# A decoder layer on one core: a second chain at the start, an earlier combine, a pipelined end, and another order of the first loads

## The chip, the cores and the metric

One core of one Trainium2 chip runs the whole kernel. Its engines work beside each other, each through its own list of instructions in order: TensorE (PE in the profile) multiplies and transposes, VectorE (DVE) and ScalarE (ACT) work on elements, GpSimd (POOL) makes masks, takes powers and issues indirect transfers, SyncE (SP) issues most other transfers. An instruction that waits for another engine or a transfer holds up everything behind it in its own list. The metric is the device time of one execution in microseconds, a median over runs.

## The reference, cut to what matters

The input x is 64 sequences of 128 tokens with 256 features; everything is float32.

```python
# 1. selective state space layer, residual twice, then a layernorm
xn = layernorm(x, gamma, beta)
x_inner, z = split(xn @ W_in, 2)              # 256 -> 2 * 512
x_conv = silu(conv1d(x_inner, conv_w) + conv_b)   # 4 taps, causal
Bmat, Cmat, delta = split(x_conv @ W_x)       # 16, 16, 1; delta = softplus
y = selective_scan(x_conv, -exp(A_log), Bmat, Cmat, delta)
y = (y + x_conv * D_skip) * silu(z)
x1 = norm(x + y @ W_out + x)
# 2. retention against a context, decay mask and rotation
qh, kh, vh = xpos(x1 @ Wq), xpos(ctx @ Wk), ctx @ Wv
x2 = norm(x1 + ((qh @ kh.T) * mask) @ vh)
# 3. experts: one shared, and 2 of 8 routed for each token
shared = (silu(x2 @ Wg) * (x2 @ Wu)) @ Wd
probs = sigmoid(x2 @ router_w.T + bias)       # top 2, scores to sum 1
routed = sum over the 2 of score * ((silu(x2 @ Wg[e]) * (x2 @ Wu[e])) @ Wd[e])
out = norm(x2 + shared + routed)
```

## The kernel before

The 64 sequences are taken in 16 groups (NG) of 4 (GB), 512 tokens to a group (T). All routed rows go through two arrays in device memory: route scatters each token's row twice into xs, sorted by expert, and the rows of products are scattered into ys by token.

What a group goes through is written as generators that yield between stretches of work. first_half(g) is front (layernorm, two transposes to xnT, the projections by w_in in two parts of four, between them the convolution on DVE and ScalarE's silu, then w_x and the softplus of delta) and scan (the selective scan as matmuls over chunks: pin and pof, pmt, the transposes to xd, the products with mt). In front, sz holds silu(z); scan multiplies it into the result, called acc. second_half(g) is after (w_out, layernorm, the retention with kh, qh and v, layernorm), route (router, top 2, places of the rows, scatters) and, when a batch of groups is complete, tile_list, which counts rows (a small product of ones and count) and lists the tiles of that batch. A tile is 256 rows (128 in the last batch) of one expert: one_tile fetches rows (rows_in<-xs) and weights, transposes, multiplies by gate and up (routed_gu), and the down product (routed_d) of the tile before; its rows go to ys. early_shared(g) is the shared expert of a group while the loop runs (L1029): hidden products, DVE's product hc, down products, the sum into x2, and a store to x2_rows.

The order of the program is made by the generators themselves: abreast takes, among several chains, always the one that is the least far on in a scale of ticks, and a chain's yield says how long its own next step should be held back. Tick g holds first_half(g), second_half(g-1), the early shared expert of g-2, and per_tick tiles of the batches listed by then (L1421). Each engine then runs its instructions in that order. A group's front waits at the free test (L632) until the group before has been read by after, because there is one sz buffer.

The seven groups in LATE (L42, groups 7 to 13) have no shared expert in the loop: route stores their x2 and its transpose, and late_shared (L1470) makes it at the end. After the loop a second abreast runs the rest of the tiles beside the shared expert of group 15, called the late tiles below, and a third, the end stage, runs late_shared for the late groups beside combine (L1242) for all 16: load the pair of product rows (picked<-ys), two adds on DVE, layernorm, store. combine runs first on the groups whose sums stand in memory.

At the start (L1536 and on) x of group 0 is loaded from POOL's queue; three small loads of A_log go on SP's, and the others on ScalarE's, w_in among the first. A comparison of A_log's rows makes a flag, and a branch (L1612 and on) picks shared_decay, which this input takes, or any_decay, which it doesn't. Exponentials of A_log (a_neg, a_row, a_col, L1587) stand on ScalarE in front of the last nine loads. After the branch, the first three steps of group 0's front are emitted (L1308), then the constants: masks on POOL, two half masks transposed on PE (L1345), the shared weights' load, tables of numbers.

layernorm (L552) is bn_stats and bn_aggr on DVE for each sequence, var, rstd on POOL, shift on DVE, and four norms on ScalarE.

Of the kernel before, what the change touches and what calls it, by code (L numbers as in the profile page):

```python
# [16 lines left out]
P = 128  # L17
# [27 lines left out]
LATE = range(7, 14)  # L45
# [8 lines left out]
def _any_decay(ctx, K):  # L54
# [77 lines left out]


    xts = [K.x0] + [const.tile([P, GB, D], F32, name=f"xt{i}") for i in range(2)]
# [375 lines left out]
def _shared_decay(ctx, K):  # L510
# [39 lines left out]
    xts = [K.x0] + [const.tile([P, GB, D], F32, name=f"xt{i}") for i in range(2)]  # L550

    def layernorm(dst, src):  # L552

        mv = small.tile([P, GB, 2], F32, name="mv")
        for b in range(GB):
            st = small.tile([P, nc.vector.BN_STATS_DIM], F32, name="st")
            nc.vector.bn_stats(st, src[:, b, :])  # L557
            nc.vector.bn_aggr(mv[:, b, :], st)  # L558
        var = small.tile([P, GB], F32, name="var")
        nc.vector.tensor_scalar(var, mv[:, :, 1], EPS, None, ALU.add)  # L560
        rstd = small.tile([P, GB], F32, name="rstd")
        nc.gpsimd.tensor_tensor(rstd, var, mhalf, ALU.pow)  # L562
        shift = small.tile([P, GB], F32, name="shift")
        nc.vector.scalar_tensor_tensor(shift, mv[:, :, 0], -1.0, rstd, ALU.mult, ALU.mult)  # L564
        yield 4.2
        for b in range(GB):
            nc.scalar.activation(  # L567
                dst[:, b, :], src[:, b, :], AF.Identity, bias=shift[:, b : b + 1], scale=rstd[:, b : b + 1]
            )
# [36 lines left out]
    def front(st):  # L606
# [3 lines left out]
        xn = one.tile([P, GB, D], F32, name="xn", tag="xn")  # L610
        yield from layernorm(xn, xt)
        yield 2.6
        xnT = one.tile([P, KD, T], F32, name="xnT", tag="xnT")
# [3 lines left out]
        xc = one.tile([P, CI, GB, L], F32, name="xc")  # L617
# [18 lines left out]
        sz = one.tile([P, CI, T], F32, name="sz")  # L636
# [15 lines left out]
        bcs = one.tile([P, T // 2], F32, name="bcs", tag="bcs")  # L652
        nc.scalar.copy(bcs, pbc)
        rows = dram.tile([2 * NS, T], F32, name="rows")
# [8 lines left out]
        tok = small.tile([P, GB, NX], F32, name="tok", bufs=1)  # L663
# [4 lines left out]
        bj = one.tile([KB, T], F32, name="bj")  # L668
        cj = one.tile([KB, T], F32, name="cj")
# [12 lines left out]
        cq = one.tile([P, GB, NS, Q], F32, name="cq", tag="xnT")  # L682
# [6 lines left out]
        raw = small.tile([P, GB], F32, name="raw", bufs=1)  # L689
        nc.vector.tensor_copy(raw, tok[:, :, NX - 1])  # L690
        e = small.tile([P, GB], F32, name="e", bufs=1)
# [3 lines left out]
        up = small.tile([P, GB], F32, name="up", bufs=1)  # L695
        nc.vector.tensor_scalar(up, e, 1.0, None, ALU.add)
        lg = small.tile([P, GB], F32, name="lg", bufs=1)
        nc.scalar.activation(lg, up, AF.Ln)

        dd = small.tile([P, GB], F32, name="dd", bufs=1)  # L700
        nc.vector.tensor_scalar(dd, up, 1.0, None, ALU.subtract)
        flat = small.tile([P, GB], F32, name="flat", bufs=1)
# [7 lines left out]
        dl = small.tile([P, GB], F32, name="dl", bufs=2)  # L710
# [3 lines left out]
    def scan(st):  # L714
# [5 lines left out]
        d1 = small.tile([P, GB, Q], F32, name="d1", bufs=1)  # L720
# [3 lines left out]
        dlb = small.tile([P, GB, 32], F32, name="dlb", bufs=1)  # L724
# [4 lines left out]
        eq = one.tile([P, GB, NS, Q], F32, name="eq", tag="xn")  # L729
# [11 lines left out]
        eb = one.tile([KB, T], F32, name="eb", tag="bcs")  # L741
# [14 lines left out]
        gq = small.tile([P, GB, Q], F32, name="gq", bufs=1)  # L756
        nc.vector.tensor_reduce(gq, eq.rearrange("p b n i -> p b i n"), AX.X, ALU.add)
        mt = one.tile([P, GB, NQ, Q], F32, name="mt", tag="dm")
# [7 lines left out]
        xd = [one.tile([P, 2, DI], F32, name=f"xd{j}", tag=tag) for j, tag in enumerate(("xnT", "xd"))]  # L766
# [21 lines left out]
    def after(g, st):  # L788
# [59 lines left out]
        x1T = one.tile([P, KD, T], F32, name="x1T")  # L848
# [61 lines left out]
    def route(g, st):  # L910
# [53 lines left out]
        rows = [st["row"], one.tile([P, GB, DX], F32, name="row1")]  # L964
# [38 lines left out]
    def shared(x2, x2T, x2s):  # L1003
# [3 lines left out]
        wd = shared_w[:, 2 * SZ :].rearrange("p (c h) -> p c h", c=CF)  # L1007
        hid = []
        for c in range(CF):
# [4 lines left out]
            hc = ring.tile([P, T], F32, name="hc", bufs=4)  # L1014
# [3 lines left out]
            yield 0.3 if c < CF - 1 else 2.0  # L1018
        for j in range(GB // 2):
            ps = gu.tile([P, 2, D], F32, name="gu")  # L1020
# [6 lines left out]
            yield  # L1027

    def early_shared(g, st):  # L1029
        yield from shared(st["x2"], st["x2T"], st["x2"])  # L1030
        nc.sync.dma_start(out=x2_rows[g].rearrange("p (b d) -> p b d", d=D), in_=st["x2"])

    def load_rows(g):
# [3 lines left out]
        return t  # L1037

# [97 lines left out]
    def fetch(i):  # L1136
# [16 lines left out]
        there.append(work[0] + 12.0)  # L1153
# [88 lines left out]
    def combine(g, x2s):  # L1242

        y = late.tile([P, GB, 2, D], F32, name="picked", bufs=3)
        nc.sync.dma_start(
            out=y, in_=ys[g * GB * 2 * L : (g + 1) * GB * 2 * L, :].rearrange(
                "(b p k) d -> p b k d", p=P, k=2)
        )
        yield 1.0
        for k in range(2):  # L1250
            nc.vector.tensor_tensor(x2s, x2s, y[:, :, k, :], ALU.add)  # L1251
        yield 3.0
        yield from layernorm(x2s, x2s)
        nc.sync.dma_start(out=out[g * GB : (g + 1) * GB].rearrange("b l d -> l b d"), in_=x2s)
# [49 lines left out]
    for before, st in zip([{"read": True}] + states, states):  # L1304
        st["free"] = lambda before=before: "read" in before
    states[0]["xt"] = xts[0]
    start = first_half(states[0])
    for _ in range(3):  # L1308
        next(start)

# [37 lines left out]
    for side in range(2):  # L1348
        t = one.tile([P, KB // NS, NS], F32, name=f"half{side}", tag="dm")
# [9 lines left out]
        ps = pm.tile([KB, P], F32, name="pm")  # L1359
        turn(ps, t.rearrange("p j n -> p (j n)"), ident)  # L1360
        tT = const.tile([KB, P], F32, name=f"halfT{side}")
        nc.vector.tensor_copy(tT, ps)
        halvesT.append(tT)
# [3 lines left out]
    shared_w = const.tile([P, 3 * SZ], F32, name="shared_w")  # L1367
    nc.sync.dma_start(out=shared_w, in_=ffn[0])
# [47 lines left out]
    for i in range(NW):  # L1416
        weights.append([const.tile([P, 2 * SZ], F32, name=f"routed_gu{i}"), const.tile([P, SZ], F32, name=f"routed_d{i}")])
    zeros = const.tile([P, DX], F32, name="zeros")
# [5 lines left out]
    for k, (groups, first, n, _) in enumerate(BATCHES[:-2]):  # L1424
        ticks = range(groups + 1, BATCHES[k + 1][0] + 1)
        for j, t in enumerate(ticks):
            per_tick[t] = n * (j + 1) // len(ticks) - n * j // len(ticks)
    def until(ready, at):
# [3 lines left out]
    def first_halves():  # L1432
        for g in range(NG):
            if g + 1 < NG:
                yield from until(lambda: g < 2 or "read" in states[g - 2], g)
                states[g + 1]["xt"] = load_x(g + 1)
            yield from placed(first_half(states[g]) if g else start, g, 54.0)
            states[g]["scanned"] = True

# [24 lines left out]
    abreast((first_halves(), True), (second_halves(), True), (shared_ones(), True), (tiles_beside(), True))  # L1464
# [5 lines left out]
    def late_shared(g):  # L1470
        x2 = load_rows(g)
        x2T = two.tile([P, KD, T], F32, name="x2T")
        nc.sync.dma_start(out=x2T.rearrange("p k t -> p (k t)"), in_=x2T_rows[g])
        yield 4.0
        x2s = late.tile([P, GB, D], F32, name="x2s_late", bufs=len(LATE))
        yield from shared(x2, x2T, x2s)
        sums.append((g, x2s))

    sums = []
# [10 lines left out]
    sums += [(g, None) for g in range(NG) if g not in LATE]  # L1490

    def all_sums():
        for i in range(NG):
            while not sums:
                yield i / NG, 1.0
            g, x2s = sums.pop(0)
            yield from placed(combine(g, load_rows(g) if x2s is None else x2s), i / NG, 12.0, 1 / NG)

    def all_shared():
        for i, g in enumerate(LATE):  # L1500
            yield from placed(late_shared(g), i / len(LATE), 27.0, 1 / len(LATE))
# [5 lines left out]
def decoder_layer(  # L1507
# [29 lines left out]
    nc.gpsimd.dma_start(out=x0, in_=x[0:GB].rearrange("b l d -> l b d"))  # L1537
# [42 lines left out]

    gam, bet = column(gamma, "gam"), column(beta, "bet")
    w_in_s = chunked(w_in, 2 * DI, "w_in_s")
    cw, cb = chunked(conv_w, TAPS, "cw"), column(conv_b, "cb")
# [105 lines left out]
```

## Time and profile before

| what | value |
| --- | --- |
| median of 3 runs | 1994.55 us (1994.12 to 1998.49) |
| the profiled execution | 1992.64 us |
| its span | 1990.8 us |
| mean granted PE clock | 0.986 |
| the late tiles, from the last batch's count to the last tile | 1516 to 1819.5 us of the span |
| the end stage | 1819.5 to 1976.3 us |
| the tail, behind the last matmul | 1976.3 to 1990.8 us |

The span is the stretch that the profile shows, from the first to the last work of the core; the execution's own time has 1.84 us around it. In the page, "PE" is the matmuls and "PEld" the loads of their stationary operand, which overlap; a float32 matmul is shown as two records. A wait names the engine that waited, the line it waited at, and what released it. In a group of records, "out<-in" are the names of the buffers.

The page's slices show the shape of the execution: PE is busy from the second slice on, DVE half the time in the loop, little among the late tiles, and more in the end stage, where the transfers are the densest:

```profile
PE   4889998999999979999999899999998999999996
DVE  3666766655565554555555645554532111113573
DMA  4111121431502123313251324152103433443772
GB/s 144 32 56 45 43 73 38 159 93 32 158 25 93 32 87 127 114 55 107 62 158 51 120 60 140 48 167 56 54 27 117 135 133 125 163 166 127 271 252 74
```

### The profile page before, as it was taken

How to read it: one execution, taken by the hardware profiler on the slowest of the kernel's cores; microseconds unless marked ns; L12 is line 12 of the kernel's file. 1: busy time of each engine (PE TensorE's matmuls, PEld its weight loads, DVE VectorE, ACT ScalarE, POOL GpSimd, SP SyncE). 2: the span in 40 equal slices, each digit the busy share in tenths (PEclk: the TensorE clock that was granted, in tenths of full speed). 3: DMA queues.
4: the chain of work that ended last, by engine and by line, in shares of the span. 5: the costliest groups of instructions: out<-in, count | busy, mean ns of one | idle time of the engine just before them, and what ended most of it. 6: DMA issues, size and time to landing. Idle time of an engine off the chain costs nothing. (4 is left out here: it accounts for less than half of the span.)

```text
span 1990.8 us, 26551 instructions
## 1 busy us (share of the span) xinstructions
PE 1873.7 (94%) x9252; PEld 1393.7 (70%) x9252; DVE 990.8 (50%) x2398; ACT 757.8 (38%) x1248; POOL 470.2 (24%) x711
## 2 busy tenths in 40 slices
PE   4889998999999979999999899999998999999996
PEld 2655665685868666767677677687776888997554
DVE  3666766655565554555555645554532111113573
ACT  3345445243434323535444434445331222222332
POOL 3031220231303031413141313131214222222010
PEclk9899999999999989999999999999999999999998
DMA  4111121431502123313251324152103433443772
GB/s 144 32 56 45 43 73 38 159 93 32 158 25 93 32 87 127 114 55 107 62 158 51 120 60 140 48 167 56 54 27 117 135 133 125 163 166 127 271 252 74
DMA packets 100775, 200.14 MB, mean 101 GB/s; under 512 B 22840, under 2 KB 60344, under 8 KB 96024
## 3 DMA queue, kind: packets, MB, share of 16 engines
q1 hardware_dynamic: 77512, 143.08, 22.9%
q0 software_dynamic: 17616, 52.46, 7.7%
q10 hardware_dynamic: 5504, 2.81, 0.5%
q8 instruction: 75, 1.23, 0.3%
q14 instruction: 68, 0.56, 0.1%
HBM read 207.33 MB, written 58.60 MB: 134 GB/s over the span
## 5 line engine op out<-in xcount | busy, mean ns | idle before, releaser
L543 PE MATMUL gu<-rows_T,routed_gu 128*128 128x256 f32 (+1 forms) x2496 | 501.9, 352 | 0.0
L543 PEld LDWEIGHTS gu<-rows_T,routed_gu 128*128 128x128 f32 x2496 | 416.7, 191 | 59.3 <-issue 16.5
L1203 DVE TENSOR_TENSOR hid<-hid,gu 128x512 f32<-128x512 f32 x135 | 92.4, 685 | 360.6 <-PE gu L543 256.6
L543 PE MATMUL pm<-routed_d,hid 128*128 128x256 f32 x1080 | 254.7, 381 | 0.3
L543 PE MATMUL pm<-xnT,w_in_s 128*128 128x512 f32 x512 | 242.0, 598 | 4.5 <-ACT xnT L580 2.7
L1219 POOL DMA_INDIRECT ys<-rows_out,to x135 | 140.8, 1043 | 406.9 <-ACT rows_out L1218 360.5
L543 PE MATMUL gu<-x2T,shared_w 128*128 128x512 f32 x512 | 229.7, 595 | 0.2
L543 PEld LDWEIGHTS pm<-routed_d,hid 128*128 128x128 f32 x1080 | 199.3, 190 | 26.4 <-issue 2.5
L628 DVE SCALAR_TENSOR_TENSOR xc<-pm,cw,xc 128x508 f32<-128x508 f32 (+2 forms) x192 | 140.9, 739 | 65.3 <-ACT xc L623 62.2
L543 PEld LDWEIGHTS gu<-x2T,shared_w 128*128 128x128 f32 x512 | 94.8, 190 | 108.4 <-issue 101.9
L543 PEld LDWEIGHTS pm<-xnT,w_in_s 128*128 128x128 f32 x512 | 95.5, 192 | 90.1 <-issue 76.6
L567 ACT ACTIVATE x<-x,shift,rstd 128x256 f32<-128x256 f32 x132 | 70.7, 592 | 204.9 <-DVE shift L564 204.9
L562 POOL TENSOR_TENSOR rstd<-var,mhalf 128x4 f32<-128x4 f32 x64 | 67.6, 1056 | 330.1 <-DVE mv L558 175.2
L1218 ACT ACTIVATE rows_out<-pm,wt 128x256 f32<-128x256 f32 x135 | 58.0, 472 | 205.3 <-PE pm L543 193.2
L543 PE MATMUL gu<-shared_w,hc 128*128 128x256 f32 x512 | 118.6, 386 | 8.1 <-DVE hc L1016 8.1
L1202 ACT ACTIVATE hid<-gu 128x512 f32<-128x512 f32 x135 | 80.4, 596 | 112.6 <-PE gu L543 102.4
L543 PE MATMUL pm<-w_out_s,sz 128*128 128x256 f32 x512 | 117.7, 382 | 5.3 <-DVE sz L784 4.9
L543 PEld LDWEIGHTS gu<-shared_w,hc 128*128 128x128 f32 x512 | 96.8, 192 | 29.7 <-DVE hc L1016 12.6
L543 PEld LDWEIGHTS pm<-w_out_s,sz 128*128 128x128 f32 x512 | 95.8, 190 | 27.6 <-DVE sz L784 9.8
L992 POOL DMA_INDIRECT xs<-x,index x64 | 66.7, 1043 | 173.4 <-DVE row L988 80.3
L623 ACT ACTIVATE xc<-pm,cb,cw 128x512 f32<-128x512 f32 x64 | 49.7, 777 | 116.7 <-PE pm L543 116.7
L1015 ACT ACTIVATE hc<-gu 128x512 f32<-128x512 f32 x64 | 37.9, 593 | 117.7 <-PE gu L543 109.6
(233 smaller groups left out, 2505.6 us busy)
## 6 DMA issues: line engine op xcount, KB each, us to landing
routed_gu<-in_ffn_dram SPq DMA_DIRECT2D x78, 1024.0 KB
routed_d<-in_ffn_dram SPq DMA_DIRECT2D x78, 512.0 KB
picked<-ys SPq DMA_DIRECT2D x16, 1024.0 KB
rows_in<-xs SPq DMA_DIRECT2D x57, 258.0 KB
cT<-in_ctxT_dram POOLq DMA_DIRECT2D x16, 512.0 KB
cq<-chunks SPq DMA_DIRECT2D x16, 512.0 KB
x_rows<-x SPq DMA_DIRECT2D x16, 512.0 KB
xt<-in_x_dram POOLq DMA_DIRECT2D x10, 512.0 KB
```

What stands on the lines that cost most here:

```text
L543: nc.tensor.matmul(out, lhsT=lhsT, rhs=rhs, **how)
L562: nc.gpsimd.tensor_tensor(rstd, var, mhalf, ALU.pow)
L567: nc.scalar.activation(dst[:, b, :], src[:, b, :], AF.Identity, bias=shift[:, b : b + 1], scale=rstd[:, b : b + 1])
L623: nc.scalar.activation(xcf[:, c, :], ps, AF.Identity, bias=cb[:, c : c + 1], scale=cw[:, c, TAPS - 1 : TAPS],)
L628: nc.vector.scalar_tensor_tensor(xc[:, c, :, s:], ps3[:, :, : L - s], cw[:, c, TAPS - 1 - s : TAPS - s], xc[:, c, :, s:], ALU.mult, ALU.add,)
L992: s = nc.gpsimd.indirect_dma_start(out=xs, in_=rows[k][:, b, :], in_offset=None, out_offset=bass.IndirectOffsetOnAxis(ap=index[:, b, k : k ...
L1015: nc.scalar.activation(hc, psg, AF.Silu)
L1202: nc.scalar.activation(hc, psg, AF.Silu)
L1203: nc.vector.tensor_tensor(hc, hc, psu, ALU.mult)
L1218: nc.scalar.activation(y[:, j, :], ps[:, j, :], AF.Copy, scale=wt[:, j : j + 1])
L1219: s = nc.gpsimd.indirect_dma_start(out=ys, in_=y[:, j, :], in_offset=None, out_offset=bass.IndirectOffsetOnAxis(ap=to[:, j : j + 1], axis=0),)
```

## The change

In parts. The late groups are 7 to 12 in place of 7 to 13, and one tile fewer is placed in the last tick of the loop:

```diff
-LATE = range(7, 14)
+LATE = range(7, 13)
...
+    per_tick[NG] -= 1
...
-        there.append(work[0] + 12.0)
+        there.append(work[0] + (12.0 if i >= NW and shape(i - NW)[0] == k else 24.0))
```

(there is when a tile's rows are taken to have landed, in the generators' own scale; it is 24 for the first three tiles of a batch.)

The second chain: group 1's first half runs beside group 0's, in buffers cut from the routed experts' weight tiles, which are not loaded yet; the first halves of later groups run one tick earlier, and sz has two buffers.

```diff
+    states[1]["own"] = {
+        "xc": weights[0][0][:, 0:2048], "xn": weights[1][0][:, 0:1024], "xnT": weights[1][0][:, 1024:2048], "xd": weights[2][0][:, 0:1024],
...
-        sz = one.tile([P, CI, T], F32, name="sz")
+        sz = one.tile([P, CI, T], F32, name="sz", bufs=2)
...
-    for before, st in zip([{"read": True}] + states, states):
+    for before, st in zip([{"read": True}] * 2 + states, states):
...
     def first_halves():
-        for g in range(NG):
+        states[2]["xt"] = load_x(2)
+        yield from placed(start, 0.0, 54.0)
+        states[0]["scanned"] = True
+        for g in range(2, NG):
             if g + 1 < NG:
-                yield from until(lambda: g < 2 or "read" in states[g - 2], g)
+                yield from until(lambda: "read" in states[g - 2], g - 1)
                 states[g + 1]["xt"] = load_x(g + 1)
-            yield from placed(first_half(states[g]) if g else start, g, 54.0)
+            yield from placed(first_half(states[g]), g - 1, 54.0)
             states[g]["scanned"] = True
+
+    def second_start():
+        yield from placed(first_half(states[1]), 0.3, 54.0)
+        states[1]["scanned"] = True
```

The start: x of group 0 is the first load on ScalarE's queue, x of group 1 stands there behind w_in and the small columns; the other loads go to SP's queue behind the first bn_stats; the exponentials that this branch needs (a_row, a_col) follow the first steps of group 0, and the half masks are transposed behind group 0's bcs.

```diff
-    nc.gpsimd.dma_start(out=x0, in_=x[0:GB].rearrange("b l d -> l b d"))
+    x1 = const.tile([P, GB, D], F32, name="x1")
+    nc.scalar.dma_start(out=x0, in_=x[0:GB].rearrange("b l d -> l b d"))
...
+    nc.scalar.dma_start(out=x1, in_=x[GB : 2 * GB].rearrange("b l d -> l b d"))
...
+    def load_rest(*behind, more=()):
+
+        for t, src in (*rest, *more):
+            with nc.allow_non_contiguous_dma(reason="vectors over partitions, once"):
+                load = nc.sync.dma_start(out=t, in_=src)
+            for name in behind:
+                tc.add_manual_dep(
+                    load.ins, name, mybir.DependencyInfo(mybir.DependencyClass.Sync, mybir.DependencyReason.DATA),
+                    reason="x comes first",
+                )
...
     for _ in range(3):
         next(start)
+    shared_w = const.tile([P, 3 * KD * FF], F32, name="shared_w")
+    K.load_rest(*first_read, more=[(shared_w, ffn[0])])
+    K.decays(a_row, a_col)
...
         nc.scalar.copy(bcs, pbc)
+        if not halvesT:
+            turn_halves()
```

The end: the shared expert is cut into shared_hidden and shared_down. A late group's down products come behind two of the next group's four hidden steps; the product rows (y) are added to x2 ahead of them; the layernorm takes two sequences at a time, and the store is in two halves. The groups that are not late are combined beside.

```diff
+    def late_shared(g, last):
+
+
+        if not loaded:
+            load_late(g)
+            yield 4.0
+        x2, x2T = loaded.pop()
+        if not last:
+            load_late(g + 1)
+        made = shared_hidden(x2T, late, 6)
+        for c in range(CF):
+            yield next(made)
+            if c == 1:
+                y = load_products(g)
+                if unsummed:
+                    yield from summed(*unsummed.pop())
...
+        unsummed.append((g, x2, y, hid))
+        if last:
+            yield 1.7
+            yield from summed(*unsummed.pop())
+
+    def summed(g, x2, y, hid):
+        for k in range(2):
+            nc.vector.tensor_tensor(x2, x2, y[:, :, k, :], ALU.add)
+        norms = []
+        for j in shared_down(x2, hid, x2, pm):
+            norms.append((j, layernorm(x2[:, 2 * j : 2 * j + 2, :], x2[:, 2 * j : 2 * j + 2, :])))
+            next(norms[-1][1])
+            yield 0.5
+        for j, norm in norms:
+            for _ in norm:
+                pass
+            store(g, x2, 2 * j, 2 * j + 2)
+        yield
...
-    sums += [(g, None) for g in range(NG) if g not in LATE]
+    early = [g for g in range(NG) if g not in LATE]
...
-            yield from placed(combine(g, load_rows(g) if x2s is None else x2s), i / NG, 12.0, 1 / NG)
+        for i, g in enumerate(early):
+            yield from placed(combine(g, load_rows(g)), i / len(early), 12.0, 1 / len(early))
```

Some buffers share memory that did not before (x1T with cT, the second row buffer of route with qh, the half masks with kh and qh), and the small helpers take buffers from the group's state.

## The prediction

> **What bounds the kernel now.** I read the page's busy times first, then a table of windows by stage, then what TensorE (PE) waited for, then short stretches of the timeline at the places named there. The page:
>
> ```profile
> PE 1873.7 (94%) x9252; PEld 1393.7 (70%) x9252; DVE 990.8 (50%) x2398; ACT 757.8 (38%) x1248; POOL 470.2 (24%) x711
> ```
>
> PE is busy 1873.7 of 1990.8 us. The change keeps every matmul and transpose and their shapes, so the 117.1 us of PE idle and the stretches at a lower clock are all it can win. Where they lie (columns: window, length, busy of PE, PEld, DVE, ACT, POOL with counts, granted PE clock, DMA share, GB/s):
>
> ```profile
> 0.00:20.30 20.30, 2.83 (x13) 1.76 (x14) 4.90 (x32) 5.37 (x10) 14.31 (x69) 1.00 0.78 215
> 20.30:47.20 26.90, 18.60 (x52) 7.68 (x51) 12.98 (x37) 13.13 (x17) 1.03 (x1) 0.95 0.26 91
> 47.20:75.00 27.80, 21.50 (x126) 18.89 (x127) 16.20 (x24) 6.53 (x11) 3.03 (x2) 0.74 0.13 33
> 75.00:345.00 270.00, 253.64 (x1220) 159.49 (x1219) 185.93 (x451) 128.81 (x199) 54.98 (x52) 1.00 0.18 51
> 345.00:730.00 385.00, 372.60 (x1814) 269.95 (x1815) 218.90 (x540) 154.36 (x249) 87.75 (x105) 0.98 0.27 83
> 730.00:1516.00 786.00, 755.22 (x3825) 576.63 (x3824) 418.60 (x1029) 327.24 (x527) 208.57 (x285) 1.00 0.29 90
> 1516.00:1819.50 303.50, 300.69 (x1762) 274.09 (x1763) 37.84 (x55) 72.65 (x144) 81.33 (x181) 0.99 0.41 134
> 1819.50:1976.30 156.80, 148.60 (x449) 85.21 (x447) 90.20 (x222) 47.61 (x89) 18.21 (x17) 0.99 0.63 220
> 1976.30:1990.80 14.50, 0.00 (x0) 0.00 (x0) 5.22 (x13) 2.07 (x4) 1.01 (x1) 0.62 0.13 42
> ```
>
> Length minus PE busy is the idle time: 17.5, 8.3, 6.3 us in the three windows of the start, 59.6 over the three of the main loop, 2.8 among the late tiles, 8.2 in the end stage, 14.5 in the tail. The third window also ran at clock 0.74. The waits that matter (us in total, times, longest):
>
> ```profile
> PE pm L543 <- DVE cj L745: 12.8, 5, 6.2
> PE pm L543 <- DVE mk L968: 12.6, 8, 4.0
> ...
> PE gu L543 <- DVE hc L1016: 8.1, 7, 2.7
> PE pm L547 <- DMA rows_in<-xs: 5.1, 2, 3.5
> PE pm L543 <- DVE d L721: 4.9, 1, 4.9
> ```
>
> And three places of the PE timeline (start us, us, operation, count, in brackets the idle time before it and its releaser):
>
> ```profile
> 717.94 2.05 PE L543 MATMUL pm<-cj,bj 128*128 128x128 f32 x8 [6.25 <-DVE cj L745]
> ...
> 724.00 0.61 PE L543 MATMUL pm<-sel,upto 128*128 128x32 f32 x2 [3.16 <-DVE mk L968]
> ...
> 1499.68 13.98 PE L543 MATMUL gu<-x2T,shared_w 128*128 128x512 f32 x32
> 1517.20 0.66 PE L547 MATMUL pm<-ident,rows_in 128*128 128x128 f32 x4 [3.54 <-DMA rows_in<-xs]
> 1519.46 1.09 PE L547 MATMUL pm<-ident,rows_in 128*128 128x128 f32 x4 [1.61 <-DMA rows_in<-xs]
> ```
>
> d is group 0's chain alone at the start; hc is the end stage's own DVE product between hidden and down; rows_in is the last batch of routed tiles, whose rows had not landed.
>
> **The change part by part.**
>
> *Start, loads.* The first x moves from POOL's queue to the head of ACT's; nine weight loads leave ACT for SP, behind the first statistics. Before, the projections (S) start at 20.26 us, and the path to it is: statistics of x at 10.03 (behind the exponentials: a_col at 8.99, with 2.37 us waited for its DMA), rstd at 12.25 with POOL, ACT busy issuing loads (0.38 to 0.53 us each) until 14.1, the norm at 14.85. Issues and exponentials leave that path. But in the changed order ACT normalises one block of x1 between x0's norm and x0's transposed copy (xnT), so xnT waits for rstd of x1, which POOL reaches only behind the rest of its constants: those from 12.25 on before sum to some 5.4 us (1.05 rstd, 0.57, 0.14, 0.19, 0.37, 0.14, 0.26, 1.42, 0.12 and the x load's 0.80). Counting on: rstd of x1 ends near 17.9, xnT 0.8 later, S near 19.6 against 20.26, a gain of 0.7. Against it: a_neg's and a_row's 640 records of 64 bytes, which decide the flag and so the branch, went at about 700 a us while alone (2.0 to 3.0 us) and about 100 a us beside x0's 4096-byte records of 160 ns. With x0 beside them from the first they land 0 to 3 us later (3: 24 big records an engine of x0 and w_in, 3.8, less the 0.9 shared before). I take 1.2, so S moves by +0.5. On SP the moved loads and shared_w, some 3.1 MB, take 14 us at the first window's 215 GB/s, ahead of chain 0's stores of bcs (41.4 before); begun by 12 us they are through by 30, so they cost nothing there. Were they not, bj and cj would come late by what is left, up to a few us.
>
> The Trainium skill, "DMA: Bandwidth & Descriptors", section "Queues, rings and completion order", says that a DMA engine takes turns between queues packet by packet; its rule speaks against putting x on a hardware queue beside the flag's loads. By it alone my estimate would be the full 3 us and a sum 1.8 worse.
>
> *Start, second chain.* Group 1's first half runs beside group 0's. Before, the products that end group 0's chain (w_out) follow S by 47.9 us. After, group 0's convolution starts some 6 us sooner (DVE no longer waits until 25.48 for group 1's x), but chain 1's ACT work and table loads (1.28 us each) and DVE's convolution stand in front of chain 0's exponentials: pin and pof come at S+35.5 against S+26.9, and DVE's list from there to the last sz, with chain 1's part in it, sums to 24.5 us, so w_out comes at about S+60.5, 12.6 later. By then PE has done of chain 1: 16 projections, 32 records of 128x512 (13.8, as in the 13.98 above), transposes 0.9, w_x 1.7, halves turned 0.2, pin and pof 1.1, pmt 0.9, xd turns 1.7: 20.3 us. Net 7.7, less 2.2 for chain 1's later waits (the cj wait was 3.74 and mt 2.56 for one chain), less S's 0.5: **-5**. Bounds: 0 (every wait of chain 1 comes back later), and -21.8 (all 14.6 us idle of windows two and three and 7.2 of half clock, 0.26 of 27.8).
>
> At the clock the row is: 4.91 us idle before d, then a mean clock of 0.74 from 47.2 to 75. The Trainium skill, "TensorE: Matmul & The Clock Gate", section "Part 1: The HAM clock gate", has half rate only after an idle window of some 3.4 us; as my waits in the changed start are of 2 to 3 us, by it the half clock would go too and my estimate would be -12 for the start, 7 lower.
>
> *Main loop.* First halves run one tick earlier, with two sz buffers, so a group's second half finds its sz a tick old: the sz wait (4.9 us, 9 times) may go, or the new order on DVE costs one more stall like the one at 717 us (6.25 and 3.16 us of waits and 13.65 us at half clock, behind a wait of 6.98 on the store x_rows<-x): -4.9 to +16. I take 0, as the chain's own DVE steps, where cj and mk come from, are the same. Group 13's shared expert and store come into ticks 15 and 16. Its PE time of 20.8 us (13.9 hidden, 6.9 down) is moved, not removed; its store makes one wait for x_rows<-x more (16.1 us in 6 such waits on DVE, mostly behind PE's other work): **+1.5**, bounds 0 and +7.
>
> *Last batch.* After the count's product PE had 13.9 us of shared work, then waited 3.54 and 1.61 for rows that landed 17.9 us after the count, with 3.4 us of half clock behind. Now a routed tile (6.9), shared hidden (13.8) and a down (3.45) follow the count, 24 us: the 5.15 us go, and half of 3.4 with them if the clock stays up: **-5**, bounds 0 and -6.9. If that order fails, the same wait stands there.
>
> *End stage.* Six late groups of 20.8 us, 124.8, in place of seven, 145.6; the seventh is the 20.8 above. What was lost was 156.8 - 145.6 = 11.2: 8.1 of hc waits and a stretch at half clock. Now the down of a group follows the next group's first hiddens, so hc is covered for all but the last group (2.7). But DVE gets denser: per group 9.3 us for a late one and 10/6 of an early sum's 4.9 (two adds of 1.22, stats 0.40 and 0.17 four times, var, shift), 17.5 of 20.8, 84%, where it was 58% of the stage; the adds of the products now stand ahead of the down's on DVE, so a late load holds the banks. Loss 8, **-3**; bounds -8.5 (only 2.7 lost) and, by the transfers' rate, +23 (rival D).
>
> *Tail.* The last late group is normed and stored in halves, but group 15's sum stands behind it on DVE, ACT and SP, with its store of 512 KB whole. Before: 1976.30 to 1984.98 and a store landing 5.8 us on. After: the same two adds, stats, norm; about 8.4 for 8.7: **-0.3**, bounds -4 (both in halves) and +3.
>
> Sum: -5 + 0 + 1.5 - 5 - 3 - 0.3 = -11.8. The profiled execution took 1992.64 us, 1.9 less than the median of the three runs, 1994.55: 1980.8 on the profile's footing, 1982.7 on the median's, rounded to **1983**.
>
> **The rivals.**
>
> *B, more.* The two chains fill the start so that the clock stays up (start -14 rather than -5: idle of the second and third window nearly gone), and the end loses 2.7 only (-8.5 rather than -3): 14.5 lower, 1968.5. For it: no idle of the start is due to loads once S is reached. Against it: DVE and ACT carry both chains there, at 13 to 16 us busy of 27 with one.
>
> *C, no change.* The start's gain is eaten on DVE (0 rather than -5), the end gives nothing (0 rather than -3): 1991; with the tail's other bound (+3), 1994. For it: PE's start work done early is only worth what later ticks don't spend waiting on the same DVE list.
>
> *D, slower.* The end stage is set by its transfers. They are 10 early groups of 2 MB and 6 late of 2.5, 35 MB, in 132.8 us (124.8 + 8): 264 GB/s. The stage gave 220 on average; 1823 to 1863 us gave 276 at a share of 0.79, which speaks against D. If it stays at 225 the stage takes 155.6, 22.8 more: 2006. It decides from 242 GB/s (35 MB in 144.6: the whole gain is gone), and is slower by over 0.2% under about 236.
>
> **How the numbers follow.** Within 0.2%, 4 us, nothing can be told from no change: 1990.6 to 1998.5. Forecast A, 1976 to 1990, 0.48; B 0.14; C 0.15; D 0.23. Faster: A, B and a fifth of C, less 0.02 for A's upper edge, 0.63. Same: the rest of C and that edge, 0.14. Slower: D, 0.23. The likeliest one's own range is 1976 to 1990. The range asked for goes from B's price to D's, 1968 to 2006; it leaves out half of D (worse rates, or the stall at 717 once more) and a third of B, about 0.16.
>
> **What would show it.** Start: the first w_out products at about 80 us with 20 us of chain 1 done, PE idle up to there under 30. Last batch: no idle before rows_in near 1500 us. End stage: hc waits at one instance, the stage 133 us, DMA near 264 GB/s, DVE's picked waits under 20 us in all. Tail: last PE to end 14 us. The prediction is wrong if the main loop's idle leaves 59.6 by more than 10 either way, or if picked waits appear in front of PE's banks.

## The result, and the profile after

The changed kernel took 1972.21 us in the median (1969.37 to 1978.22, 4 runs) against 1994.97 (1994.12 to 1998.49, 4 runs): ratio 0.9885, 95% interval 0.9862 to 0.9907, or 22.8 us less. The profiled execution took 1972.62 us with a span of 1970.8.

The table of windows, cut at the events of the prediction's table (first projections, the counts of batches 1, 2 and the last, last tile, last matmul) and, early on, at 60 and 105 us (columns: window, length, busy of PE, PEld, DVE, ACT, POOL, granted PE clock, DMA share, GB/s):

```profile
0.00:23.80 23.80, 2.31 (x10) 1.24 (x10) 7.07 (x41) 4.98 (x10) 13.77 (x68) 1.00 0.82 250
23.80:60.00 36.20, 36.16 (x108) 16.42 (x108) 19.51 (x34) 23.33 (x31) 2.48 (x2) 1.00 0.16 43
60.00:105.00 45.00, 36.73 (x251) 30.82 (x250) 37.12 (x77) 22.15 (x36) 5.44 (x6) 0.89 0.17 43
105.00:366.40 261.40, 250.35 (x1210) 157.81 (x1209) 179.20 (x443) 128.05 (x192) 56.09 (x51) 1.00 0.18 51
366.40:735.00 368.60, 360.90 (x1753) 258.93 (x1751) 204.45 (x508) 148.60 (x242) 79.35 (x100) 0.99 0.27 84
735.00:1501.00 766.00, 738.32 (x3710) 569.33 (x3700) 391.86 (x955) 306.05 (x500) 195.61 (x269) 0.98 0.28 89
1501.00:1824.00 323.00, 321.86 (x1836) 286.49 (x1837) 48.33 (x115) 77.86 (x153) 94.93 (x198) 1.00 0.42 138
1824.00:1957.00 133.00, 128.03 (x393) 73.26 (x392) 89.01 (x223) 43.59 (x83) 23.06 (x22) 1.00 0.69 235
1957.00:1970.80 13.80, 0.07 (x1) 0.00 (x0) 3.80 (x17) 3.90 (x8) 1.70 (x2) 0.68 0.25 82
```

PE is idle 96.1 us (1970.8 less 1874.7) in place of 117.1. The start is full from 23.8 to 60 us, but begins 3.5 us later. The waits of PE (us in total, times, longest):

```profile
PE pm L549 <- ACT xn L595: 17.8, 12, 8.3
PE pm L545 <- DVE cj L775: 9.2, 4, 6.2
PE ps L1663 <- DVE others L1660: 7.1, 1, 7.1
PE pm L545 <- ACT xnT L608: 6.9, 3, 6.0
...
PE gu L545 <- DVE hc L1045: 3.8, 3, 2.1
...
PE pm L545 <- DVE dlb L755: 1.7, 2, 1.5
PE pm L545 <- DVE mk L998: 1.4, 2, 0.7
```

rows_in is no longer among them; mk fell from 12.6 to 1.4 and dlb from 9.8 to 1.7; cj stayed at one batch start (6.2 us). Others grew: sel from 2.4 to 6.3, and x1T (5.0) and x (4.9) are new.

Idle time doesn't show what a lower clock or a gap between records costs, so the rest is read by one more sum: for each matmul record the median spacing of its shape in the trace of before (0.429 us for 128x512, 0.216 for 128x256, 0.112 for 128x128, and so on) is its work, 1825.4 us in all for every kernel here, and the time that passed less the work issued by then is what was lost. The differences between the rows are what the table is good for. Lost us by stretch, of each profiled execution:

| kernel | to 105 | 105 to 800 | 800 to 1100 | 1100 to 1440 | 1440 to 1815 | end stage | tail |
| --- | --- | --- | --- | --- | --- | --- | --- |
| before | 43.8 | 47.7 | 17.8 | 21.8 | 7.2 | 12.1 | 15.0 |
| changed | 41.0 | 49.4 | 7.2 | 24.8 | 1.7 | 7.3 | 14.1 |
| set 1: u_chain | 39.5 | 56.5 | 17.5 | 20.4 | 1.5 | 8.6 | 14.3 |
| u_tick | 41.4 | 46.3 | 17.3 | 19.5 | 1.6 | 7.7 | 14.2 |
| u_late | 41.1 | 49.9 | 7.0 | 20.9 | 5.0 | 7.4 | 10.1 |
| u_end | 40.6 | 48.7 | 7.6 | 21.4 | 1.7 | 11.4 | 23.7 |
| set 2: c_sz | 40.3 | 60.5 | 12.1 | 13.6 | 0.3 | 7.8 | 13.8 |
| t12 | 41.2 | 39.1 | 7.1 | 12.6 | 7.9 | 6.2 | 10.1 |
| x0pool | 38.7 | 42.0 | 7.1 | 17.8 | 6.7 | 7.1 | 9.9 |
| xnT_first | 35.5 | 44.4 | 6.8 | 18.5 | 3.4 | 5.8 | 10.1 |
| set 3: after_b | 39.5 | 45.6 | 7.0 | 16.3 | 0.3 | 8.2 | 14.3 |
| there12 | 41.0 | 39.8 | 7.4 | 15.0 | 10.6 | 8.7 | 13.9 |
| t12_b | 40.8 | 39.4 | 7.8 | 13.3 | 7.0 | 6.5 | 9.9 |
| best | 36.3 | 35.8 | 7.2 | 13.8 | 7.3 | 6.3 | 10.0 |

From the first two rows the 20 us between the two profiled executions are: 2.8 at the start, 6.0 in the loop from 105 to 1440 (10.6 gained between 800 and 1100, some 4.7 given back around it), 5.5 at the last batch, 4.8 in the end stage, 0.9 in the tail. The rows under them are the experiments. u_end and the changed kernel have the same work and order up to the end stage and differ by 3.7 us in the loop, so a difference in the loop is good to no better than some 4 us on one chip, and the changed kernel's own two traces, on two chips (changed and after_b), differ by 12.5 there; the tail and the stretch from 800 to 1100 repeat within 1 us where the order is the same.

### The profile page after: what moved, and what is told of

It reads as the page before. It is cut to its first block, busy times and chain, and to the rows that moved or that the text cites. A ratio compares the mean times of both kernels' runs of the same rounds, so it can differ in the third digit from the quotient of the medians.

```text
span 1970.8 us, 26601 instructions
## 1 busy us (share of the span) xinstructions
PE 1874.7 (95%) x9252; PEld 1394.3 (71%) x9252; DVE 980.4 (50%) x2409; ACT 758.5 (38%) x1247; POOL 472.4 (24%) x715
## 3 DMA queue, kind: packets, MB, share of 16 engines
q1 hardware_dynamic: 80424, 143.72, 23.3%
## 4 chain that ended last, share of the span: by engine, by line
PE 42%; DVE 3%; issue 2%; DMA 1%; ACT 1%; POOL 1%; SPq 0%; POOLq 0%; DVEq 0%; ACTq 0%
PE gu L545 20%; PE pm L545 19%; PE pm L549 2%; DMA picked<-ys 1%; POOL rstd L590 1%; DVE st L583 0%; DVE x L1299 0%; ACT x L595 0%; DVE xt L1299 0%; DVE hc L1045 0%; DVE eq L783 0%; DVE mv L586 0%; ACT xn L595 0%; DVE gq L787 0%; DVE x_late L1564 0%
## 5 line engine op out<-in xcount | busy, mean ns | idle before, releaser
L545 PEld LDWEIGHTS gu<-rows_T,routed_gu 128*128 128x128 f32 x2496 | 416.4, 191 | 59.6 <-issue 16.8
L545 PE MATMUL pm<-xnT,w_in_s 128*128 128x512 f32 x480 | 227.3, 600 | 7.0 <-ACT xnT L608 6.9
L1271 POOL DMA_INDIRECT ys<-rows_out,to x135 | 135.6, 1004 | 285.7 <-ACT rows_out L1270 252.5
L595 ACT ACTIVATE x<-x,shift,rstd 128x256 f32<-128x256 f32 x156 | 81.8, 590 | 227.9 <-DVE shift L592 227.9
L590 POOL TENSOR_TENSOR rstd<-var,mhalf 128x4 f32<-128x4 f32 (+1 forms) x70 | 74.5, 1064 | 389.4 <-DVE var L588 338.0
L656 DVE SCALAR_TENSOR_TENSOR xc<-pm,cw,xc 128x508 f32<-128x508 f32 (+1 forms) x180 | 132.0, 738 | 53.6 <-ACT xc L651 52.1
L545 PEld LDWEIGHTS pm<-xnT,w_in_s 128*128 128x128 f32 x480 | 90.3, 192 | 85.9 <-issue 72.0
L545 PEld LDWEIGHTS pm<-w_out_s,sz 128*128 128x128 f32 x512 | 95.5, 190 | 16.3 <-issue 2.6
L583 DVE BATCH_NORM_STATS2 st<-x 128x6 f32<-128x256 f32 x200 | 78.1, 408 | 1.9 <-DVE flag L1664 0.8
L1226 ACT COPY rows_T<-pm 128x512 f32<-128x512 f32 (+1 forms) x78 | 40.9, 525 | 82.7 <-PE pm L549 73.4
L545 PE MATMUL gu<-shared_w,hc 128*128 128x256 f32 x320 | 72.5, 380 | 0.0
```

The source lines that it names most:

```text
L545: nc.tensor.matmul(out, lhsT=lhsT, rhs=rhs, **how)
L583: read_by = nc.vector.bn_stats(st, src[:, b, :])
L590: nc.gpsimd.tensor_tensor(rstd, var, mhalf[:, 0:n], ALU.pow)
L595: nc.scalar.activation(dst[:, b, :], src[:, b, :], AF.Identity, bias=shift[:, b : b + 1], scale=rstd[:, b : b + 1])
L656: nc.vector.scalar_tensor_tensor(xc[:, c, :, s:], ps3[:, :, : L - s], cw[:, c, TAPS - 1 - s : TAPS - s], xc[:, c, :, s:], ALU.mult, ALU.add,)
L1226: nc.scalar.copy(tT, ps)
```

## The experiments

The three sets ran on different chips, and the kernel before took 1994.2, 1976.6 and 1979.4 us on them. Times are therefore compared inside a set, or by the ratio to the kernel before. Set 1 has no run of the changed kernel of its own: it stands beside the 1972.2 us from above, where the kernel before took 1995.0.

**Set 1, one part undone at a time.** u_chain takes the second chain out, and with it the earlier tick and the second sz buffer:

```diff
-    for before, st in zip([{"read": True}] * 2 + states, states):
+    for before, st in zip([{"read": True}] + states, states):
...
-            yield from placed(first_half(states[g]), g - 1, 54.0)
+            yield from placed(first_half(states[g]) if g else start, g, 54.0)
...
-        sz = one.tile([P, CI, T], F32, name="sz", bufs=2)
+        sz = one.tile([P, CI, T], F32, name="sz")
```

> The changed kernel with its second chain undone: group 1's first half no longer runs beside group 0's, every first half starts a tick later, one sz buffer as before; loads, combine and pipelined end stay changed. By the traces the changed kernel gained 2.5 us up to 105 us and 6 us more from there to the last batch's count. If both belong to the second chain (theory): 8 to 9 us slower than the changed kernel, about 1981, and PE's waits for dlb and sz come back in the loop (9.8 and 4.9 us before). If the loop's part came from the moved shared expert, tile and batch starts (rival): 2 to 3 us slower, about 1975, without those waits.

1986.22 us (1982.22 to 1989.68), ratio 0.9960 (0.9945 to 0.9974): 14 us over the changed kernel's 1972.2. The two theories both took the start for a gain; the table says otherwise. Up to 105 us u_chain lost less (39.5 against 41.0), and the loop from 105 to 1440 lost 94.4 against 81.4. Of these 13 us 10.3 lie between 800 and 1100, where waits for dlb (4.5), sz (2.6) and mk (2.1) are back, and 7.1 from 105 to 800, at the starts of batches; 4.4 come back behind 1100. The two longest waits before 700 us have no like in the changed kernel, whose longest near these places are 2.87 and 2.43 us:

```profile
364.66 2.07 PE L545 MATMUL pm<-xnT,w_in_s 128*128 128x512 f32 x2 [7.23 <-ACT xnT L608]
...
531.33 2.08 PE L545 MATMUL pm<-cj,bj 128*128 128x128 f32 x8 [5.10 <-DVE cj L775]
```

u_tick keeps the chain at the start and puts the later first halves back by a tick:

```diff
-            yield from placed(first_half(states[g]), g - 1, 54.0)
+            yield from placed(first_half(states[g]), g - (g < 5), 54.0, 2.0 if g == 4 else 1.0)
```

> The changed kernel with the second chain kept at the start and both sz buffers, but group 4's first half stretched over two ticks and the first halves from group 5 on one tick later, where they stood before. Theory (first halves a tick ahead loosen the loop): the start's 2.5 us stay, the loop's 6 us go, about 1978, waits for dlb and mk return. Rival (the tick's place is nothing, two sz buffers or the rest do it): within 2 us of the changed kernel, about 1972.

1973.08 us (1971.86 to 1975.15), ratio 0.9892 (0.9877 to 0.9908): the rival by time. But the trace shows the theory's waits where it put them, and less lost elsewhere, which pays for them. PE's waits from 800 to 1100 us, first in the trace of before, then in u_tick, then in the changed kernel:

```profile
PE pm L543 <- DVE dlb L725: 6.1, 4, 1.7
PE pm L543 <- DVE mk L968: 2.1, 3, 0.7
PE pm L543 <- DVE sz L784: 2.1, 3, 0.7
```

```profile
PE pm L545 <- DVE dlb L755: 5.9, 4, 1.8
PE pm L545 <- DVE sz L814: 2.2, 4, 0.7
PE pm L545 <- DVE mk L998: 2.1, 3, 0.7
```

```profile
PE pm L549 <- ACT xn L595: 1.0, 3, 0.6
PE pm L545 <- DVE mk L998: 0.7, 1, 0.7
```

With the first half a tick ahead these steady waits of some 10 us go (and the stretch loses 7.2 us in place of 17.3). In exchange u_tick lost 3.1 us less from 105 to 800 and 5.3 less from 1100 to 1440. No one stall accounts for it: u_tick had none at 391 and 552 us, where the changed kernel waited 2.87 and 2.43 with half clock behind, but one of 2.54 at 337, and around 715 and 743 it waited 6.7, 3.2 and 3.4 us where the changed kernel waited 6.2 and 2.0 (742 and 768).

u_late makes seven groups late again and gives the loop its tile back:

```diff
-LATE = range(7, 13)
+LATE = range(7, 14)
...
-    per_tick[NG] -= 1
```

> The changed kernel with group 13 late again (groups 7 to 13) and the loop's last tile back; the pipelined end and the second chain stay. Theory (the moved shared expert and tile cover the last batch's rows): the wait for rows_in of about 5 us behind the last count returns with some half clock, and the rest is nothing as the 20.8 us of PE only move: 1977 to 1979. Rival (the cover came from the later landing time that the order assumes for a batch's first tiles): no wait there, within 2 us of the changed kernel. The end stage then has 7 groups of 20.8 us and DVE is less dense there, at best 1 us gained.

1967.53 us (1962.68 to 1969.86), ratio 0.9860 (0.9842 to 0.9879): 4.7 us faster than the changed kernel, outside both, though the two intervals of the ratios overlap a little. No wait of 5 us for rows_in came back (the longest there was 1.07), though the stretch from 1440 lost 5.0 for 1.7 (2.42 of it in a wait for a tile's weights, routed_gu, at 1567); and the tail fell from 13.8 to 9.5 us behind the last matmul, since now the last late group's second half ends the kernel. The end of the changed kernel, for comparison (start, us, instruction, count, idle before and releaser):

```profile
1960.53 1.09 ACT L595 ACTIVATE x_late<-x_late,shift,rstd 128x256 f32<-128x256 f32 x2 [2.79 <-DVE shift L592]
...
1962.66 2.07 ACT L595 ACTIVATE x<-x,shift,rstd 128x256 f32<-128x256 f32 x4 [1.04 <-DVE shift L592]
1964.76 0.37 SPq L1086 DMA_DIRECT2D out_dram<-x  x1
```

The halves of the last late group are normed by 1961.6; the four norms and the whole store of group 15 come behind and set the end.

u_end puts the end stage back as it was, with six late groups:

```diff
-        made = shared_hidden(x2T, late, 6)
...
+        hid = yield from shared_hidden(x2T, ring, 4)
+        yield 1.7
+        for _ in shared_down(x2, hid, x2s, gu):
+            yield
+        sums.append((g, x2s))
```

> The changed kernel with the end stage as before: down behind the same group's hiddens, sums behind, layernorm and store whole; six late groups as changed. Theory (pipelining covers DVE's hc and is what the end gained): 5 to 6 us slower, about 1978, with hc waits of 1 to 2.7 us at six places. Rival (the end gained by having one late group fewer): within 2 us, about 1972 to 1974.

1984.73 us (1982.32 to 1991.04), ratio 0.9961 (0.9946 to 0.9976): 12.5 us slower, twice the theory. PE was done at the same time (1957.3 against 1957.1), with 4.1 us more lost in the stage; the rest came behind it:

```profile
1820.00:1957.00 137.00, 129.33 (x394) 74.69 (x392) 79.11 (x189) 37.98 (x70) 14.99 (x14) 0.99 0.66 229
1957.00:1980.50 23.50, 0.27 (x2) 0.00 (x0) 11.56 (x41) 10.37 (x20) 4.84 (x4) 0.57 0.39 137
```

Sums, norms and stores of several groups were still to do when PE stopped, 23.3 us for 13.8. The old end sums all 16 groups, here beside six late ones where the kernel before had seven; that this is why it no longer fits beside PE's work is argued and not tested. So 12.5 us is what the new end is worth with this set of late groups, not against the kernel before, whose own end had lost 12.1 and a tail of 15.0.

**Set 2.** c_sz is u_chain with only the two sz buffers kept, t12 is u_late with the assumed landing time at 12, x0pool and xnT_first change the start of u_late:

```diff
-            there.append(work[0] + (12.0 if i >= NW and shape(i - NW)[0] == k else 24.0))
+            there.append(work[0] + 12.0)
...
-    nc.scalar.dma_start(out=x0, in_=x[0:GB].rearrange("b l d -> l b d"))
+    nc.gpsimd.dma_start(out=x0, in_=x[0:GB].rearrange("b l d -> l b d"))
...
+            if nth == 2:
+                tc.add_manual_dep(
+                    normed.ins, first_turned[KD - 1],
...
```

> The second chain undone as in u_chain (1986 us), but with the two sz buffers, so that a group's z projections need not wait until the group before is read. Theory (the double buffer loosens the loop and is what the chain part gained there): 1974 to 1977, dlb and sz waits mostly gone. Rival (it is the work of group 1 done early, and that first and second halves of different groups lie further apart, that loosens the loop): 1984 to 1987, waits as in u_chain.

1970.98 us (1965.90 to 1978.30), ratio 0.9973 (0.9960 to 0.9986), close to u_chain's 0.9960, with intervals that overlap: the rival. The sz wait is gone from 800 to 1100 us, dlb is there with 6.1 us and mk with 2.1; and the waits of 7.2 and 5.1 us at two batch starts are there as in u_chain (370 and 536 us). A second buffer alone gains nothing that the ratio shows; the table's loop is 8.2 us below u_chain's, but on another chip.

> u_late (seven late groups, 1967.5 us) with the assumed landing time of a batch's first tiles back at 12 in place of 24. Theory (that number, not group 13's shared expert, took the wait behind the last count away): PE waits some 5 us for rows_in near 1500 us again, 1972 to 1974. Rival (it plays no part): 1966 to 1969 and no such wait.

1949.16 us (1946.97 to 1951.29), ratio 0.9859 (0.9842 to 0.9876), as u_late's. The waits for rows_in came back (5.3 us in 3, of which 1.7 near 750 and the rest behind the last count) and 7.9 us were lost from 1440, yet the time did not rise. Set 3 takes this up.

> u_late (1967.5 us) with x of group 0 on POOL's queue again; all else of the changed loads stays. Theory (x at the head of ScalarE's queue holds up the small loads of A_log, flag at 7.4 us for 4.9): the flag comes 2 to 2.5 us earlier and the first projections with it, 1965 to 1966. Rival (x0 then lands later or the flag is late for another load, w_in): no change, 1967 to 1968.

1956.28 us (1954.18 to 1960.68), ratio 0.9899 (0.9882 to 0.9916). The flag did not come sooner: its cast stands at 7.78 us, at 7.38 in the changed kernel and 4.89 before. But the run swapped one large load for another: w_in, issued at 1.88 us before and at 1.31 in the changed kernel, now goes out at 0.80, and x0 behind it. The transfers in the traces show it. Of the 640 records of 64 bytes that the flag needs, 510 began between 2 and 3 us in the kernel before, with no large record beside them, and the last at 3.7. In the changed kernel 319 began in that time, beside x0's records (2.1 to 4.5 us) and then w_in's, and the last at 6.2; in x0pool 197, beside w_in's (2.2 to 5.9), and the last at 6.4, when x0's first had gone at 5.8. So the flag is late with either load beside it. To hold both back wasn't tried.

> u_late (1967.5 us) with one order more: ScalarE's norm of group 1 waits until group 0's xnT is written. Theory (xnT waits some 4 to 6 us for POOL's rstd of group 1): the first projections start near 19 us in place of 23.8, and the whole gain stays: 1963 to 1964. Rival (the start is held by DVE and ScalarE of two chains later on, so an earlier start only lengthens a later wait): 1966 to 1968.

1954.66 us (1952.00 to 1956.51), ratio 0.9892 (0.9877 to 0.9906), 1.6 us under x0pool, whose interval overlaps. The first projections came at 18.0 us in place of u_late's 24.8 and the start lost 35.5 us in place of 41.1. As u_late was not run on this chip, its own worth is read from set 3.

**Set 3.** The changed kernel again, the landing time alone undone in it, t12 again, and t12 with xnT first:

> The changed kernel once more, beside the three others of this set on one chip, since the kernel before took 1994 us on the chip of the first set and 1977 on that of the second, so that times of different sets can't be compared. Ratio to the kernel before as at first, 0.986 to 0.991.

> The changed kernel with one number undone: the assumed landing time of a batch's first tiles at 12 again. Theory (that number puts group 13's work and a routed tile ahead of the fetch, and so covers the last batch's rows): 4 to 6 us slower than after_b, a wait of 2 to 5 us for rows_in near 1500 us. Rival (12 is the better number, since it takes a stall at other batches away, as t12's trace has no stalls near 391 and 552 us): 4 to 7 us faster than after_b.

> t12 again (seven late groups, landing time 12), beside after_b on one chip. If both parts are worth what the sets before say (4.7 us for the late groups, some 5 for the landing time): 9 to 11 us faster than after_b. If the second set's lower time was its chip alone: 4 to 5 us faster.

> t12 with group 1's norm on ScalarE held behind group 0's xnT. Theory (the first projections come 5 us sooner and the gain stays): 4 to 5 us faster than t12_b. Rival (the loop gives it back at the first batch, where PE waits for other things): within 2 us of t12_b.

| kernel | median us | range | ratio | 95% interval |
| --- | --- | --- | --- | --- |
| after_b | 1961.00 | 1958.32 to 1967.15 | 0.9918 | 0.9894 to 0.9941 |
| there12 | 1960.71 | 1959.25 to 1963.44 | 0.9909 | 0.9888 to 0.9931 |
| t12_b | 1950.50 | 1950.06 to 1954.72 | 0.9863 | 0.9838 to 0.9887 |
| best | 1947.77 | 1944.02 to 1948.70 | 0.9842 | 0.9817 to 0.9866 |

after_b's ratio, 0.9918, lies just above the 0.986 to 0.991 that was expected.

there12 against after_b, no difference in time, was neither theory's number and both theories' mechanism: the wait is back, and larger than in the kernel before, behind the last count,

```profile
1501.38 1.12 PE L549 MATMUL pm<-ident,rows_in 128*128 128x128 f32 x4 [8.22 <-DMA rows_in<-xs]
```

so 10.6 us are lost from 1440 in place of 0.3; and the stretch from 105 to 800 lost 39.8 in place of 45.6, that from 1100 15.0 for 16.3. The stalls at 391 and 552 us (2.86 and 2.37 in after_b) are gone, but one of 3.44 stands at 367, and the wait of 6.73 us at 741 became three of 1.53, 2.47 and 1.94 between 732 and 756. The one number buys the last batch's cover and pays for it at the starts of the batches before.

t12_b against there12 differs in group 13 and a tile: 10.2 us faster, with 4.0 us in the tail, 3.6 from 1440 and 2.2 in the end stage. So moving group 13 out of the end was a loss: clearly here, and by 4.7 us on the first chip, where the intervals overlap. Against after_b t12_b is 10.5 us faster, as its first case said, but not by that case's parts: there12 puts the landing time at nothing and group 13 at 10.2.

best against t12_b: 2.7 us, between theory and rival, with ranges that don't overlap, of the 5.8 us by which the first projections are earlier. PE in best:

```profile
15.29 2.12 PE L549 MATMUL pm<-ident,xn 128*128 128x128 f32 x8 [7.89 <-ACT xn L597]
18.07 10.73 PE L545 MATMUL pm<-xnT,w_in_s 128*128 128x512 f32 x20 [0.65 <-ACT xnT L616]
```

best is the fastest here: 13.2 us under the changed kernel on the same chip and 31.6 under the kernel before.

## Why the prediction was right, and where it was not

The sign and the range held (1972.2 in 1968 to 2006); the forecast of 1983 was half of the gain, and the time lies under the likeliest case's own range; that the range held owes something to its width, 38 us. Of the 8.2 us between the 20.0 gained in the two traces and the 11.8 of the sum, 7.5 are the loop (-6.0 for 0) with group 13's +1.5 in it; the end stage, the tail and the last batch gained 2.9 more than forecast, and the start 2.2 less.

**Start, -5 with S at +0.5: measured -2.8 with S at +3.5.** Both mechanisms that the prediction named against it were there, larger than taken. The flag chain's release came 2.5 us later (PE waited 7.1 us for it, 4.7 before; 1.2 was taken, with bounds of 0 and 3), and by the mechanism that the prediction gave, small records beside large ones: the records counted under x0pool show it. And xnT waited for group 1's norm:

```profile
14.99 2.08 ACT L595 ACTIVATE xn<-x,shift,rstd 128x256 f32<-128x256 f32 x4 [3.58 <-DVE shift L592]
22.49 0.60 ACT L595 ACTIVATE routed_gu<-x,shift,rstd 128x256 f32<-128x256 f32 x1 [5.43 <-DVE shift L592]
23.00 1.43 ACT L608 ACTIVATE xnT<-pm,bet,gam 128x512 f32<-128x512 f32 x2
```

Here the second line is group 1's first norm: it holds xnT, ready to be copied from 17.8 us (the transposes' end), until 23.0. xnT_first and best show the cause. The prediction had seen this wait and counted it too short: POOL's rstd of x1 ended at 22.3 us, not near 17.9. Its masks began 2.5 us later, behind the flag (8.2 for 5.8), and group 2's x was issued ahead of it (20.2 to 21.2, behind 1.6 us of idle). (The terms listed for POOL add to 5.1, not 5.4, and the loads that left ScalarE's queue are ten, not nine.)

The second chain did gain what it should behind S: the loss to 105 us less the time of S is 17.2 us in the changed kernel, 23.5 before and 21.6 in u_chain, and 17.5 and 18.2 in xnT_first and best; the first w_out products came at 82.3 us with 27.9 us of PE idle up to there, as the prediction's signs had it (80, under 30). But it cost 5.9 us ahead of S (23.8 for u_chain's 17.9, where nothing stands before xnT), so that u_chain lost 1.5 us less by 105. The new order of the loads, put at a loss of 0.5 with that wait in it, gained 2.4 us without the chain (20.3 to 17.9 us).

**Main loop, "I take 0, as the chain's own DVE steps, where cj and mk come from, are the same": measured -6.0.** This is the step that failed, and the prediction's own sign of being wrong, PE's idle in the loop more than 10 away from 59.6, came: from 75 us to the last count it is 48.7. The DVE steps are the same, but the group that PE can turn to while they run is not: with first halves a tick ahead, dlb, mk and sz are ready before PE comes to them (11 us of waits fell to 3 from 800 to 1100 us). Only the sz wait was in the bound (4.9). u_chain puts the second chain, with its tick and its buffer, at some 14 us, nearly all of it in the loop; its part outside the steady ticks lies in stalls at batch starts, which fell differently in each order, and what decides them wasn't isolated. u_tick shows that such differences can outweigh the steady gain: with the waits back, its time was the same. And the -6.0 is a net: the new landing time, to which the prediction gave no price in the loop, cost some 7 us there by there12 (54.8 lost from 105 to 800 and 1100 to 1440, for 61.9). Both sizes are near what two traces can differ by.

**Group 13, moved at +1.5, bounds 0 to 7: 4.7 and 10.2.** The forecast priced the store's wait; what it cost was the tail that a full set of early sums leaves behind, and cover in the stage.

**Last batch, -5: measured -5.5.** Right in size; the order of that stretch was read correctly, but the cover hangs on the landing time, which the prediction didn't name. Group 13's work without it waits 8.22 us for rows_in (there12); the landing time without group 13 waits 1.07 (u_late), though 5.0 us are lost there in all; both together lose 1.7 and 0.3.

**End stage, -3: measured -4.8.** hc waits fell from 8.1 to 3.8 us (in three places, where the forecast had one), and the stage took 133.0 us, the forecast's 132.8. The term was right, its loss put at 8 for 7.3.

**Tail, -0.3: measured -0.9.** Group 15's sum ended the kernel as said; u_late shows that 4 us were to be had.

Of the rivals, B asked for a start at full clock and 2.7 us lost at the end: neither came; the time is near B's for another reason. C fell with the loop. D did not come: DVE's waits for picked in the end stage were 3.6 us in all, at 235 GB/s in the stage, under the 242 where D was to decide; the window moved 31 MB in its 133 us, not 35, so the others must lie outside it, and 242 was not the right mark.

On the clock, the Trainium skill, "TensorE: Matmul & The Clock Gate", section "Part 1: The HAM clock gate", asks for an idle window of some 3.4 us before the rate is halved. This case's trace disagrees: in the changed kernel a wait of 2.43 us at 552 was enough, as the windows before and behind it show by their clock:

```profile
540.00:552.00 12.00, 9.63 (x77) 8.14 (x75) 4.47 (x15) 6.79 (x8) 5.13 (x7) 1.00 0.60 162
552.30:555.70 3.40, 3.40 (x15) 3.22 (x15) 3.40 (x6) 0.69 (x1) 1.92 (x2) 0.51 0.55 178
```

So the -12 that the rule would have made of the start did not come: the third window still ran at 0.89, with waits of 2.65 and 2.47 us in it.

## What to carry to other kernels

Where PE is bound by order and not by work, price a schedule's shift in the steady ticks too: sum the small recurring waits (6 us in 4, 2 us in 3) over the stretch, and ask what PE has to turn to when its turn at them comes, not only whether the waited-for steps change. But don't take that sum for the gain: the stalls at batch starts move with the order, and in u_tick they and what else moved cancelled 10 us of it. Where two chains share an engine that runs in order, look for the first instruction of the second chain that stands before a short step of the first; one added order was worth 2.7 us. And when work leaves a final stage, check what then stands last: moving 20.8 us of PE work out of it cost 10 us on one chip and some 5 on another.

## What was not expected of the hardware

The kernel before took 1994, 1977 and 1979 us on three chips, a spread of 0.9%. The changed kernel's two traces differ by 5.9 us in PE's busy time (1874.7 and 1868.8) and most in the loop, 81.4 and 68.9 us lost. Why one chip stalls less wasn't settled. The ratio of the same pair of kernels came out as 0.9885 and 0.9918, with intervals that just overlap, so parts worth a few us are best told apart on one chip.
